# The first attention of layer 1 by sorted keys, ranks and indirect DMA in place of 512x512 numerators

## The chip, the core and the metric

The kernel runs on one core of one Trainium2 chip. The metric is the device time of one execution in microseconds, the median of the runs given; a separate, profiled execution supplies the trace. All times below are microseconds unless a row says ns.

## The reference

Input x is 32 samples of 512 nodes with 256 features; one adjacency matrix, 512x512, serves all of them. Four graph layers follow, each adding its result to x after a layer norm and a ReLU. Layer 0 is a masked attention of 4 heads, layer 2 a graph attention of 4 heads, layer 3 one of 8 heads with a prior. Layer 1, cut to what matters here:

```python
o1 = relu(h @ mlp1_w + mlp1_b)              # 512 nodes x 512 features
h1 = o1 @ W_fc
f1, f2 = h1 @ a[:512, 0], h1 @ a[512:, 0]
e = leaky_relu(f1[:, :, None] + f2[:, None, :], 0.2)   # no mask
att = softmax(e, axis=2)
out = elu(elu(att @ h1)) + o1
o3 = relu(out @ mlp2_w + mlp2_b)
# then a second graph attention of o3, masked by adj, and a residual
```

The first attention has no mask and its score depends on f1[i] + f2[j] alone. Leaky ReLU has two branches: for the nodes j with f2[j] > -f1[i] the numerator is exp(f1[i] + f2[j]), for the others exp(0.2 (f1[i] + f2[j])). Each is a product of a factor of i and a factor of j. With the nodes sorted by f2, every output row is therefore a suffix sum of one kind of weighted rows plus a prefix sum of the other, cut at the place where f2 passes -f1[i].

## The kernel before, in words

Everything is fp32; two masks are kept in bf16. A tile of 128 partitions by 512 columns is a "block" (a pool of 60), a PSUM bank holds as much (8 of them), and a sample's x is 128 x 4 x 256 (a pool of 5).

The 32 samples are not looped over on the chip. The program records the steps of all samples (class Plan, line 82 on), prices each with the function cost (line 333), and schedules them by hand: a list scheduler (order, line 169) puts every step on its engine's queue in the order of its modelled start, with due times that follow from PERIOD, the tuned numbers in URGENT, and the earliest starts in STARTS, PACE and LAYERS. At most AHEAD = 4 samples run past the oldest. What comes out is one fixed order for each of the five queues: PE (matmuls), DVE, ACT, POOL (GpSimd) and SP (which issues most DMAs). Each queue runs in order; an instruction that waits holds up all behind it. All planned instructions have line 297 in the profile, so groups are told apart by tile names.

A sample goes through these steps:

- norm_t: statistics on DVE, a power on POOL (`rs`), normalised rows `h` on ACT, eight transposes on PE, a ReLU on ACT (`hT`).
- layer 0: projections, score pairs (`sc`, two row tiles of 64 at once), Exp on ACT, mask on DVE, weighted sums in column tiles. In normalise the sums go through DRAM: `sums` to `s1` to `few`, a reciprocal, `s2`, and `rc` broadcast back.
- layer 1, first attention (first_gat). The values v = o1 W_fc are computed node by node, with f1 and f2 as two more columns (`sd`). The largest f2 is found; ew holds a factor per node for each branch; r1 spreads the i factor over all partitions. Then DVE makes the numerators p1[j, i] = max(r[i] * ew1[j], ew0[j]), four 128x512 blocks, sums them (`total`), and PE transposes the sums to get 1/sum (`rs1`, `rc`). Sixteen matmuls of 128 x 128 by 512 columns multiply v by p (`av`). elu2 applies the two ELUs with three ACT and three DVE passes over each of four blocks.
- layer 1, second attention (second_gat): masked, with numerators from ACT and DVE.
- layers 2 and 3 (separable): a row of scores per head goes to DRAM (`rd<-rT`) and comes back on all partitions (`R`, 256 KB each, 12 a sample). For each head ACT computes Exp(R + e), DVE takes a maximum and the mask (`p`), PE sums in column tiles. The sums over j are made on DVE (`total`), for one group of heads in layer 3 by POOL DMAs that add (`p<-p`).

After the last sample a few tests on the weights decide whether the result stands (`go`); otherwise a second, general program runs.

Of the kernel before, what the change touches and what calls it, by code (L numbers as in the profile page):

```python
# [14 lines left out]
I32 = mybir.dt.int32  # L15
AF = mybir.ActivationFunctionType
# [4 lines left out]
P = 128  # L21
# [20 lines left out]

PERIOD = 107.0
STARTS, PACE = (0.0, 4.0, 19.0, 123.0), 101.0
LAYERS = (0.0, 32.0, 34.0, 184.0)

URGENT = {
    "stats:0": -231, "mv:0": -37, "rs:0": -123, "ms:0": -205, "h:0": 11, "pt:0": -750, "hT:0": 14, "mm:0": -216,  # L50
    "sc:0": -122, "p0:0": -65, "total:0": -98, "av:0": 34, "sums:0": -578, "s1:0": 49, "few:0": -6, "s2:0": 16,
    "rc:0": -235, "oT:0": 85, "mv:1": -1, "rs:1": -312, "ms:1": 79, "h:1": -294, "pt:1": -8, "hT:1": 210, "o1:1": 230,
    "sd:1": -3, "v1:1": 496, "nd:1": -243, "ew:1": 150, "p1:1": 192, "total:1": -170, "sm:1": 80, "rs1:1": -271,
    "rc:1": 295, "av:1": -43, "y:1": -155, "e:1": -181, "o2:1": 223, "o3:1": 97, "v2:1": -74, "sd2:1": 230,
    "mn:1": -599, "None:1": 532, "ew2:1": 73, "p2:1": 326, "rs2:1": -12, "u:1": 67, "x:1": 261, "stats:2": 253,
    "mv:2": -2, "ve:2": -111, "rs:2": 9, "ms:2": 327, "h:2": -217, "pt:2": 246, "hT:2": -176, "mm:2": -27,
    "vs:2": -140, "es4:2": -547, "e4:2": 121, "rd:2": -46, "R:2": 10, "p3:2": -509, "av:2": -104, "total:2": -557,
    "sm:2": 273, "r4:2": -73, "ue:2": -350, "x:2": -11, "stats:3": -7, "mv:3": -124, "ve:3": 186, "rs:3": 271,
    "ms:3": -493, "pt:3": 488, "hT:3": -507, "mm:3": -191, "vs:3": -282, "es8:3": 187, "e8:3": -10, "rT:3": -676,
    "rd:3": 450, "R:3": 367, "p3:3": -733, "av:3": -428, "total:3": 545, "sm:3": -50, "sums:3": 213, "raw:3": 11,  # L60
    "s1:3": 84, "s2:3": 121, "rc:3": -208, "oT:3": 42, "None:3": 359, "af:3": 10, "top:3": 409, "ok:3": 38,
    "values:3": -217, "rows:3": 208, "gp:3": -60, "gram:3": -190, "gab:3": 123, "sq:3": -31, "tp:3": -40,
    "res:3": 224,
}
BLOCKS, KEEP = 60, 2
# [16 lines left out]
class Plan:  # L82
# [11 lines left out]
    OWN = dict(block=8, bank=2)  # L94
    SPARE = dict(block=2, bank=1)
# [28 lines left out]
    def add(self, attribute, engine, op, args, kw):  # L124
# [11 lines left out]
        reads = [v for v in list(args) + list(kw.values()) if isinstance(v, bass.AP) and not any(v is w for w in writes)]  # L136
        for ap, writing in [(v, False) for v in reads] + [(v, True) for v in writes]:
            if ap.tensor.name not in self.tile_tag:
                continue
            name, box = ap.tensor.name, extent(ap)  # L140
            if name not in step.touches:
                step.touches.append(name)
            record = self.history.setdefault(name, [])
            for other, obox, owriting in record:
                bank = writing and owriting and step.engine == other.engine == "PE"
                if (writing or owriting) and other is not step and (bank or overlap(box, obox)):
                    if other not in step.before:
                        step.before.append(other)
                        other.after.append(step)
            record.append((step, box, writing))  # L150
# [182 lines left out]
def cost(engine, op, args, kw, out):  # L333
# [22 lines left out]
    if engine == "POOL":  # L356
        if op == "dma_start":
            return 1.1, (5.2 if n == N else 8.0)
        return (1.0 if n < 16 else 0.683), 0.1
# [7 lines left out]
def gnn_stack_kernel(ctx: ExitStack, tc: tile.TileContext, a: dict, out: bass.AP):  # L367
# [47 lines left out]
    spread = const.tile([P, B], F32, name="spread")  # L415
    bq8 = const.tile([P, KD], F32, name="bq8")
# [23 lines left out]
    with prep_stack, tc.manual_schedule():  # L440
# [21 lines left out]
        nc.vector.memset(ones, 1.0)  # L462
        adjf = prep.tile([P, NT, N], F32, name="adjf", bufs=1)
# [133 lines left out]
    def pipelined(stack):  # L597
# [4 lines left out]
        q = Plan(nc, PERIOD)  # L602
        def block(name):

            return q.tile(big, [P, N], name, BLOCKS, keep=KEEP, tag="block")
# [7 lines left out]
        def small(name, *free):  # L613
            return q.tile(big, [P, *free], name, 4)

# [187 lines left out]
        def first_gat(o1):  # L803

            va, vb, sd = blocks("v1", 2), blocks("v1", 2), small("sd", NT, 2)
            for t in range(0, NT, 2):
                for i, ps in enumerate((bank("mm"), bank("mm"))):
                    for k in range(KH):
                        q.tensor.matmul(ps[:, : D + 2], o1[k][:, col(t + i)], wfc[:, k, D:], start=(k == 0), stop=(k == KH - 1))
                    q.scalar.copy(sd[:, t + i, :], ps[:, D : D + 2])  # L810
                    q.scalar.copy(half(vb, t + i), ps[:, :D])
            for t in range(0, NT, 2):
                q.scalar.copy(T(va[t // 2], "p (t d) -> p t d", d=D), node_major2(wfc[:, :, :D], t, o1))
            nd = largest(sd[:, :, 1])
            ew = small("ew", 3, NT)
            q.vector.tensor_scalar(ew[:, 2, :], sd[:, :, 0], nd[:, 0:1], 0.0, op0=ALU.add, op1=ALU.max)
            q.scalar.activation(ew[:, 2, :], ew[:, 2, :], AF.Exp, scale=ALPHA - 1.0)
            q.scalar.activation(ew[:, 0, :], sd[:, :, 1], AF.Exp, bias=nd[:, 1:2])
            q.scalar.activation(ew[:, 1, :], sd[:, :, 1], AF.Exp, bias=nd[:, 2:3], scale=ALPHA)
            r, p = on_all("r1", ew[:, 2, :]), blocks("p1", NT)  # L820
            for j in range(NT):
                q.vector.tensor_scalar(p[j], r, ew[:, 1, j : j + 1], ew[:, 0, j : j + 1], op0=ALU.mult, op1=ALU.max)
            rc = inverse_sums(p)
            o2 = blocks("o2", KH)
            for m in range(KH):
                elu2(o2[m], weighted([half(va if m < 2 else vb, j)[:, col(m % 2)] for j in range(NT)], p), rc, o1[m])
            return o2

        def second_gat(o3, xt):

            v, sd = q.tile(big, [P, NT, D + 1], "v2", 2), small("sd2", NT, 2)
            for t in range(NT):
                ps = node_major(wh, t, o3, 0, D + 2)
                q.scalar.activation(v[:, t, :D], ps[:, :D], AF.Identity, bias=ones[:, 0:1])
                q.scalar.copy(sd[:, t, :], ps[:, D : D + 2])
            q.vector.memset(v[:, :, D : D + 1], 1.0)
# [13 lines left out]
            for t in range(0, NT, 2):  # L850
                e, u, avs, rs = block("e"), block("u"), [], small("rs2", 2, 2)
                for i in range(2):
                    av = bank("av")
                    avs.append(av)
                    for j in range(NT):
                        q.tensor.matmul(
                            av[:, : D + 1], p[j][:, col(t + i)], v[:, j, :], start=(j == 0), stop=(j == NT - 1)
# [34 lines left out]
        def separable(xt, w, nh, mask, bars):  # L892
# [13 lines left out]
            rT = q.tile(big, [P, P], "rT", 4, tag="turned")  # L906
# [85 lines left out]
        def tests():  # L992
# [8 lines left out]
            for t in range(NT):  # L1001
                ai, af = q.tile(big, [P, N], "ai", BLOCKS, keep=KEEP, tag="block", dtype=I32), block("af")
# [56 lines left out]
        for i in range(B):  # L1059
# [12 lines left out]
            lambda n: big.tile([P, N], F32, tag="block", name=n, bufs=BLOCKS),  # L1072
# [3 lines left out]
        with tc.manual_schedule():  # L1076
# [6 lines left out]
            nc.vector.tensor_tensor(go1, go1, narrow[:1, :], op=ALU.mult)  # L1083
            nc.vector.tensor_copy(go, go1)

    def general(stack):
# [35 lines left out]
        small = stack.enter_context(tc.tile_pool(name="small", bufs=4))  # L1122
# [375 lines left out]
```

## Time and profile before

| | us |
|---|---|
| median of 3 runs | 3902.6 (3900.93 to 3904.77) |
| the profiled execution | 3905.73 |
| its span, first to last instruction | 3903.9 |
| PE busy | 3824.9 |
| DVE busy | 3292.2 |
| ACT busy | 2837.1 |
| POOL busy | 519.1 |
| DMA moved | 292.65 MB, mean 75 GB/s |

How to read the lines below: a group is "line engine operation out<-in, partitions x elements, xcount | busy us, mean ns of one | idle before, and what ended it". A stage row gives the stretch, its length, then busy time and count of PE, PEld (weight loads), DVE, ACT and POOL, the granted clock of PE, the share of the 16 DMA engines in use, and GB/s. A DMA queue row gives packets, MB, and the time of its packets as a share of 16 engines' span. Short instructions of PE overlap in the records, so the distance from one start to the next says more of a matmul than its mean. An fp32 matmul leaves two records.

### The profile page before, as it was taken

The numbers are of one execution on the slowest core, as the hardware profiler recorded it, in microseconds if no ns is written. First come the engines' busy times: TensorE is split into PE (matmuls) and PEld (weight loads), VectorE is DVE, ScalarE is ACT, GpSimd is POOL, SyncE is SP. The second block draws the span as 40 slices with busy tenths as digits, with TensorE's granted clock in tenths as the row PEclk, the third lists the DMA queues.
The fourth block names the chain that finished last, engine by engine and source line by source line (L and its number), as shares of the span: only waits on it lengthen the run. The fifth ranks groups of instructions, "written<-read, shape, count | busy, mean of one in ns | idle before, by whom it ended". The sixth has DMA issues, their size and how long they took to land.

```text
span 3903.9 us, 53766 instructions
## 1 busy us (share of the span) xinstructions
PE 3824.9 (98%) x17400; PEld 2230.5 (57%) x17400; DVE 3292.2 (84%) x7177; ACT 2837.1 (73%) x6128; POOL 519.1 (13%) x530
## 2 busy tenths in 40 slices
PE   8999999999999999999999999999999999999996
PEld 4555565555566555566565556565655555655643
DVE  5578988888988888988889988889888889888896
ACT  4567777777777767777677777677777777776784
POOL 0001110111110111110111111111101111101110
PEclk9999999999999999999999999999999999999998
DMA  3012331323332333332333323333323333314241
GB/s 100 19 48 61 88 93 52 92 61 82 88 84 59 93 61 82 87 76 67 82 63 89 89 66 78 81 63 88 93 58 85 70 73 88 88 55 94 46 110 48
DMA packets 217623, 292.65 MB, mean 75 GB/s; under 512 B 49915, under 2 KB 103422, under 8 KB 217334
## 3 DMA queue, kind: packets, MB, share of 16 engines
q0 software_dynamic: 68864, 111.18, 16.5%
q1 hardware_dynamic: 148196, 177.69, 14.6%
q8 instruction: 140, 2.29, 0.3%
q14 instruction: 149, 1.22, 0.1%
q10 hardware_dynamic: 274, 0.26, 0.0%
HBM read 158.79 MB, written 19.10 MB: 46 GB/s over the span
## 4 chain that ended last, share of the span: by engine, by line
PE 85%; ACT 8%; DVE 3%; issue 2%; DMA 2%; POOL 0%; SPq 0%; DVEq 0%; ACTq 0%; POOLq 0%
PE mm L297 43%; PE av L297 31%; PE pt L297 6%; ACT p L297 6%; PE sm L297 3%; DVE p L297 2%; PE sc L297 1%; DMA p<-p 1%; ACT h L297 1%; DVE total L297 1%; POOL rs L297 0%; DMA rc<-s 0%; DVE x L297 0%; DMA s<-few 0%; DVE rc L297 0%
## 5 line engine op out<-in xcount | busy, mean ns | idle before, releaser
L297 ACT ACTIVATE p<-R,e 128x512 f32<-128x512 f32 x1536 | 1001.5, 716 | 82.5 <-DVE total L297 75.6
L297 DVE SCALAR_TENSOR_TENSOR p<-p,e,mask3T 128x512 f32<-128x512 f32 x1024 | 715.0, 746 | 12.9 <-ACT p L297 12.9
L297 PE MATMUL av<-p,v 128*64 128x512 f32 (+1 forms) x2048 | 697.7, 597 | 6.6 <-ACT v L297 5.4
L297 DVE TENSOR_TENSOR total<-total,p 128x512 f32<-128x512 f32 x808 | 511.3, 686 | 0.1
L297 PE MATMUL av<-p,vs 128*32 128x512 f32 (+1 forms) x3072 | 497.9, 596 | 5.9 <-DVE p L297 5.9
L297 POOL TENSOR_TENSOR rs<-ve,mhalf 128x4 f32<-128x4 f32 x128 | 155.5, 1220 | 2367.8 <-DVE few L297 858.5
L297 POOL DMA_DIRECT2D p<-p x360 | 342.9, 1314 | 934.3 <-PE av L297 790.4
L297 PE MATMUL mm<-W_fc,o 128*128 128x256 f32 (+1 forms) x2048 | 459.5, 380 | 0.4 <-ACT o L297 0.4
L297 PEld LDWEIGHTS av<-p,v 128*64 128x64 f32 (+1 forms) x2048 | 257.6, 163 | 334.5 <-issue 278.1
L297 PEld LDWEIGHTS mm<-W_fc,o 128*128 128x128 f32 x2048 | 384.9, 190 | 83.3 <-issue 22.7
L297 DVE SCALAR_TENSOR_TENSOR p<-p,e,mask1T 128x512 f32<-128x512 f32 x512 | 352.8, 746 | 10.3 <-ACT p L297 10.1
L297 DVE TENSOR_TENSOR p<-p,mask0T 128x512 f32<-128x512 f32 x512 | 317.8, 686 | 13.9 <-ACT p L297 13.9
L297 ACT ACTIVATE h<-x,ms,rs 128x256 f32<-128x256 f32 x512 | 271.4, 593 | 69.9 <-DVE ms L297 69.8
L297 PEld LDWEIGHTS av<-p,vs 128*32 128x32 f32 (+1 forms) x3072 | 138.6, 119 | 310.0 <-issue 263.1
L297 DVE TENSOR_TENSOR total<-p,p 128x512 f32<-128x512 f32 x404 | 267.4, 690 | 39.0 <-PE av L297 22.6
L297 ACT ACTIVATE p<-sc 128x512 f32<-128x512 f32 x512 | 254.4, 673 | 3.7 <-PE sc L297 1.1
L297 PE MATMUL mm<-w,hT 128*128 128x272 f32 (+1 forms) x1024 | 253.5, 396 | 1.3 <-ACT hT L297 1.3
L297 PE MATMUL av<-v,p 128*128 128x257 f32 x1024 | 232.6, 380 | 2.7 <-ACT o L297 1.4
L297 PE MATMUL mm<-o,mlp_w 128*128 128x512 f32 x512 | 230.3, 593 | 2.1 <-DVE o L297 2.1
L297 PE MATMUL mm<-hT,mlp_w 128*128 128x512 f32 x512 | 230.9, 593 | 1.0 <-ACT hT L297 1.0
L297 PE MATMUL sc<-qT,kT 64*128 64x512 f32 x1024 | 228.9, 596 | 0.0
L297 ACT ACTIVATE e<-av,ones,rs 128x256 f32<-128x256 f32 x128 | 65.6, 562 | 220.8 <-PE av L297 108.6
(187 smaller groups left out, 5783.1 us busy)
## 6 DMA issues: line engine op xcount, KB each, us to landing
R<-rd SPq DMA_DIRECT2D x384, 256.0 KB
p<-p POOLq DMA_DIRECT2D x360, 256.0 KB, 4.9
x<-in_x_dram SPq DMA_DIRECT2D x32, 512.0 KB
x<-boa POOLq DMA_DIRECT2D x32, 512.0 KB, 6.5
rc<-s SPq DMA_DIRECT2D x128, 128.0 KB
out_dram<-x SPq DMA_DIRECT2D x32, 512.0 KB
rc<-s SPq DMA_DIRECT2D x248, 64.0 KB
s<-sums SPq DMA_DIRECT2D x94, 8.0 KB
```

Source lines behind the costliest of these rows:

```text
L297: getattr(getattr(self.nc, attribute), op)(*args, **kw)
```

## The change

The first attention no longer builds numerators. The values are written row-wise (two halves of 256 columns plus 1, then f1 and f2) into four blocks of 514 columns. The f2 of all nodes is spread over all partitions by four transposes. Eight Sign passes on ACT with summed output count, for each node, how many f2 lie below its own (its rank) and how many exceed -f1 (its cut). Four indirect DMAs on POOL scatter the rows to DRAM in rank order; SP reads them back sorted. Sums are then taken in half blocks of 64 rows: a 64x64 triangle times the weights (`w`) is multiplied with the sorted rows (`put`), in row-tiled pairs, giving within each block the suffix sums of one branch and the prefix sums of the other. ACT copies each pair's result out (`tab`) and SP writes it to a DRAM table of 513 rows, both branches side by side; the sums of the weights alone go there as single elements. The block totals are read back (`tot`), a 0/1 matrix picks the blocks before and behind the cut, and a matmul of 16 rows adds them up (`behind`). Two indirect DMAs for each of four tiles gather a table row per node by its cut; one of them adds to what is there. DVE and ACT divide and apply the ELUs row-wise, and 16 transposes bring the result back to feature-major.

A test is added that all ranks are different (`ranks`), else the general program runs. The planner prices an indirect DMA at 1.5 on POOL and 5.5 to land, and treats the two DRAM tensors as one piece each (a reader waits for all writers). The numbers of the plan are new. Blocks become 514 columns wide, and there are 62. In second_gat the values move into two such blocks.

```diff
-PERIOD = 107.0
-STARTS, PACE = (0.0, 4.0, 19.0, 123.0), 101.0
-LAYERS = (0.0, 32.0, 34.0, 184.0)
+HALF = 64
+ROW = 2 * D + 1
+PERIOD = 135.0
+STARTS, PACE = (0.0, 0.0, 7.0, 47.0), 112.0
+LAYERS = (0.0, 39.0, 87.0, 208.0)
...
-BLOCKS, KEEP = 60, 2
+BLOCKS, KEEP = 62, 2
...
+    SHARED = ("sorted", "sums_of")
...
+                if shared:
+                    clash = writing != owriting
...
+        if op == "indirect_dma_start":
+            return 1.5, 5.5
...
         def first_gat(o1):
-            va, vb, sd = blocks("v1", 2), blocks("v1", 2), small("sd", NT, 2)
...
-            r, p = on_all("r1", ew[:, 2, :]), blocks("p1", NT)
-            for j in range(NT):
-                q.vector.tensor_scalar(p[j], r, ew[:, 1, j : j + 1], ew[:, 0, j : j + 1], op0=ALU.mult, op1=ALU.max)
-            rc = inverse_sums(p)
-            o2 = blocks("o2", KH)
-            for m in range(KH):
-                elu2(o2[m], weighted([half(va if m < 2 else vb, j)[:, col(m % 2)] for j in range(NT)], p), rc, o1[m])
...
+            for t in range(NT):
+                q.tensor.transpose(pt[:, col(t)], rows[t][:, 2 * D + 1 :].to_broadcast([P, P]), ident)
+            q.vector.reduce_max(nd[:, 0:1], pt, axis=AX.X)
...
+            for i, scale in enumerate((-1.0, 1.0)):
+                for t in range(NT):
+                    q.scalar.activation(
+                        w, pt, AF.Sign, bias=rows[t][:, 2 * D + 1 - i : 2 * D + 2 - i], scale=scale,
+                        accum_out=sg[:, i, t : t + 1],
+                    )
...
+            order = q.tile(dram, [N, 2 * D + 2], "order", 6, tag="sorted")
+            for t in range(NT):
+                q.gpsimd.indirect_dma_start(
+                    out=whole(order), out_offset=bass.IndirectOffsetOnAxis(ap=at[:, 0, t : t + 1], axis=0),
+                    in_=rows[t], in_offset=None, bounds_check=N - 1, oob_is_err=False,
+                )
...
+            q.sync.dma_start(ds_, T(order[:, 2 * D + 1 :], "(t p) c -> p (t c)", p=P))
+            put = blocks("v1s", NT)
+            for t in range(NT):
+                q.sync.dma_start(put[t], order[t * P : (t + 1) * P, : 2 * D])
...
+            q.vector.tensor_tensor(
+                T(w, "p (t i c) -> p t i c", t=NT, i=2), tri[:, None, :, :].to_broadcast([P, NT, 2, HALF]),
+                T(ab, "p i t -> p t i")[:, :, :, None].to_broadcast([P, NT, 2, HALF]), op=ALU.mult,
+            )
...
+            table = q.tile(dram, [N + 1, 2 * ROW], "table", 6, tag="sums_of")
...
+            for i in range(2):
+                r = slice(i * HALF, (i + 1) * HALF)
+                q.scalar.copy(sums[r], T(sm[r, :16], "p (s i t) -> p i t s", s=2, i=2)[:, i])
+                q.sync.dma_start(
+                    of(ROW + i * (2 * ROW - 1), [2 * ROW, HALF], [HALF * 2 * ROW, 2 * NT], [1, 1]),
+                    T(sums[r], "p t s -> p (t s)")[:, :, None],
+                )
...
+            for t in range(NT):
+                tt = [bank("av"), bank("av")]
+                with q.unit("rows", 0.86):
+                    for s in range(2):
+                        r = slice(s * HALF, (s + 1) * HALF)
+                        q.tensor.matmul(tt[s], w[r, col(t)], put[t][r, :], start=True, stop=True)
+                for s in range(2):
+                    b = block("tab")
+                    q.scalar.copy(b, tt[s])
+                    q.sync.dma_start(of((2 * t + s) * HALF * 2 * ROW + ROW + 1, [2 * D, 2], [2 * ROW, HALF], [1, 2 * D]), b)
...
+            for t in range(NT):
+                q.sync.dma_start(
+                    tot[32 * t : 32 * t + 16, :],
+                    of(ROW + 1, [HALF * 2 * ROW - ROW - 1, 2], [HALF * 2 * ROW, 8], [1, 2 * D]),
+                )
+            behind = [bank("av") for _ in range(NT)]
+            with q.unit("rows", 0.86):
+                for t in range(NT):
+                    r = slice(32 * t, 32 * t + 16)
+                    q.tensor.matmul(behind[t], wt[r, :], tot[r, :], start=True, stop=True)
+            for t in range(NT):
+                g.append(wide("g1"))
+                pick = dict(
+                    out_offset=None, in_=whole(table), bounds_check=N, oob_is_err=True,
+                    in_offset=bass.IndirectOffsetOnAxis(ap=at[:, 1, t : t + 1], axis=0),
+                )
+                q.gpsimd.indirect_dma_start(out=g[t], element_offset=2 * D, **pick)
+                u.append(block("u1"))
+                q.scalar.copy(u[t], behind[t])
+                q.gpsimd.indirect_dma_start(out=u[t], compute_op=ALU.add, **pick)
...
+                q.vector.scalar_tensor_tensor(f, g[t][:, 2:], ew[:, 0, t : t + 1], f, op0=ALU.mult, op1=ALU.add)
+                q.scalar.activation(e, f, AF.Relu, bias=ones[:, 0:1], scale=rs[:, 1, t : t + 1])
+                q.scalar.activation(e, e, AF.Exp, scale=-1.0)
+                q.scalar.activation(e, e, AF.Exp, bias=mone)
+                q.vector.scalar_tensor_tensor(f, f, rs[:, 0, t : t + 1], e, op0=ALU.mult, op1=ALU.max)
+            o2 = blocks("o2", KH)
+            for m in range(KH):
+                pt = bank("pt")
+                for t in range(NT):
+                    q.tensor.transpose(pt[:, col(t)], u[t][:, col(m)], ident)
+                q.vector.tensor_tensor(o2[m], pt, o1[m], op=ALU.add)
             return o2
```

## The prediction

> **What bounds the kernel now.** I read the page's busy shares first, then the stage table, the waits, and the groups by shape inside ten periods.
>
> ```profile
> PE 3824.9 (98%) x17400; PEld 2230.5 (57%) x17400; DVE 3292.2 (84%) x7177; ACT 2837.1 (73%) x6128; POOL 519.1 (13%) x530
> ...
> q0 software_dynamic: 68864, 111.18, 16.5%
> q1 hardware_dynamic: 148196, 177.69, 14.6%
> ```
>
> TensorE is busy almost throughout; the 16 DMA engines have about 31% of work. In the chain of work the same PE piece (mm, 16 records, 6.87 us) starts at 1509.27 and again at 1626.87, so I cut ten periods of 117.6 us out of the steady part:
>
> ```profile
> 1509.27:2685.27 1176.00, 1168.69 (x5328) 685.67 (x5331) 1020.08 (x2216) 878.43 (x1905) 163.82 (x167) 1.00 0.33 77
> ```
>
> Columns: length, then PE, PEld, DVE, ACT, POOL busy. Per sample: PE 116.9 of 117.6, DVE 102.0, ACT 87.8, POOL 16.4. The clock is 1.00. So one sample costs what its matmuls cost; 32 x 117.6 = 3763, and the other 141 us of the 3903.9 span are the pipeline's head and tail (PE's largest single wait, 25.5 us in all, is for ACT h). The profiled execution took 3905.7, 1.8 more than its span and 3.1 more than the median.
>
> **What the change takes from PE.** Ten periods hold:
>
> ```profile
> L297 PE MATMUL av<-p,v 128*128 128x512 f32 x320 | 142.7, 593 | 1.0 <-ACT v L297 1.0
> ...
> L297 PE MATMUL sm<-ident,total 128*128 128x128 f32 x40 | 6.0, 273 | 0.0
> L297 PE MATMUL pt<-ident,rs 128*128 128x128 f32 x40 | 6.0, 273 | 0.0
> ```
>
> An fp32 matmul leaves two records, so 320 are 16 matmuls a sample. In the order of time 24 of them take 10.30 us to the next instruction, 0.86 a matmul: 13.7 us a sample. Thirteen transposes also go (sums, their spread, r1, the maximum), 0.11 apart in a run: 1.4. Removed: 15.1.
>
> Added, per sample: four row-tiled pairs, 64 rows each, at the 0.88 of the score pairs, which have that shape (32 records in 7.07 us): 3.6. Four 16-row matmuls on four row groups: 0.9 if they run together as the four 32-column `sm` matmuls do (8 records in 0.9), 3.4 if one by one; I take 0.9, since the layout is the same turned round. Four matmuls of 8 columns at 0.22 (the eight one-column matmuls of L540 leave 16 records in 1.8 us): 0.9. Twenty-one transposes at 0.11: 2.3. Changes of array mode: 0.5, an estimate (four at the 0.13 that lies free ahead of the first score pair at 1573.86). Sum 8.2. Net: 7 us a sample off PE, 224 in all.
>
> **What it adds to DVE and ACT.** DVE loses 14.0 (four p at 0.55, three totals and a reduction at 0.69, twelve y/o passes at 0.69, small ones) and gains 15.6 (eight scalar_tensor_tensor at 0.75, four PSUM adds, w and the maximum at 0.69, some 35 small ones at 0.15 to 0.23): about 103.5. ACT loses 13 and gains 28: eight Sign passes at 0.7 to 0.8 (row `p<-R,e` 716 ns, plus the sum written out), twelve copies at 0.58, eight biased 256-column copies at 0.49, the exponentials as before: about 102. In a period of 110.6 both would be at 92 to 94%. Nothing before shows three engines so full; between 0 and 6 us a sample lost to their in-order queues I take 2, because DVE at 87% cost PE only 0.7 us. Without other losses: 3903.9 - 224 + 64 + some 15 for a longer tail = 3759 of span.
>
> Bounding the unseen: Sign could need another table than Exp (each load 1283 ns in the page's ACT rows, two or more a sample), but Relu, Identity, Copy and Exp alternate here with no load between; I take 0.
>
> **POOL.** Twelve indirect DMAs a sample are new. Nearest rows: an ordinary 128-row DMA there.
>
> ```profile
> 1506.39 3.57 POOL L297 DMA_DIRECT2D p<-p  x4 [23.99 <-PE av L297]
> 1510.22 0.89 POOL L297 DMA_DIRECT2D p<-p  x1 [0.25 <-DVE total L297]
> ```
>
> By these 0.9 to 1.3 each, 11 to 16 us a sample on an engine with 16.4 of 117.6 used. [...] I take 1.5, by the row.
>
> **DMA: where I expect the loss.** Bytes are no problem: about 17 us a sample of work on each of the 16 engines (160 rows of 2 KB for scatter, reads and gathers at 0.1, half that again for the adding ones at 0.18, 1536 four-byte pieces). The eight `tab` writes are different. Each stores 128 rows of 2 KB, and its DRAM side is [2, 64, 512], outermost count 2. Two candidates for their price. By size the row is `R<-rd`: 256 KB, 128 packets of 2 KB at 84 (median) to 101 ns (mean) over 16 engines, under 1 us. By shape it is this one:
>
> ```profile
> rd<-rT SPq DMA_DIRECT2D x32, 8.0 KB
> rd<-rT SPq DMA_DIRECT2D x32, 16.0 KB
> ```
>
> Its DRAM side has 4 token blocks outermost. In the trace's packet records every DMA ends with one four-byte packet per engine it used: a load of x leaves 16, the 16 KB `rd<-rT` at 1583.0 leaves 4, and its 32 packets of 25 to 42 ns take 0.30 us, some 3.2 at a time. [...] So I take the row by shape: 64 rows x 84 to 101 ns = 5.4 to 6.5 us a DMA, and since all eight share two engines, 43 to 52 us a sample one after the other. With the 36.6 those engines have now (31.1% of 117.6), the 17, and the reads of `tot` (also 2 engines, 3), they would be busy 100 to 109 us of a period: not above it, but a queue.
>
> What waits: the reads of `tot` (SP), the gathers (POOL), by whole tensor, so for the last `tab`. Behind the wait on SP's in-order queue stand R, s, few and rc of the other samples; on POOL the `rs` power of every norm and the `p<-p` sums; on PE the `behind` matmuls and all after them. The plan prices each `tab` at 0.4 + 3.4 + 1.4 us side by side; with eight copies at 0.58 before them it expects the table about 10 us after the first copy. With 43 to 52 of own work, stretched by other traffic on those engines, I put the real end at 55: 45 late. How much the static order absorbs is read from a chain of before: the exponentials of ew end at 1617.7, PE turns them at 1626.2, 9 us; R that landed at 1586 to 1595 is first used at 1592.3, later heads wait up to 20. So 5 to 20 at a hop; over the two or three hops here 10 to 30; I take 17. Left: 28 us a sample that PE stands still (10 to 40). It comes back every period, since nothing lets PE pass a waiting instruction.
>
> Removed waits go nowhere useful: the old chain (r1, totals, sums, rc) cost PE almost nothing.
>
> **Sum.** Period 117.6 - 7 + 2 + 28 = 140.6; x 32 = 4499; head and tail 141 + 15: 4655 of span. Outside it 1.8, against the median -3.1: about 4650.
>
> **Rivals.**
> 1. *The table writes stall everything* (forecast, 55%): 4650; with 15 to 42 us left, 4240 to 5100.
> 2. *PE gets its 7 us* (29%): 3757. The writes spread over more engines than the row by shape says, or the order leaves some 40 us between table and use. For it: PE is the bound today, and each sample lives some 585 us between load of x and store (load at 1576.8 follows the store of five samples before at 1573.9), so there is queueing to be eaten. It decides when less than 5 us of lateness is left over. Against it: the four packets of `rd<-rT`. Range 3650 to 3880.
> [...]
> 4. *The chain's other hops or full ACT and DVE eat the gain* (8%): 7 to 15 us a sample lost, 3900 to 4100.
>
> **Numbers.** This kernel's measurement tells about 0.2% from no change. Slower: 55 + 8 + 6 (of case 4) = 69%; same 3% (2 of case 4, 1 of case 2); faster 28%. Likeliest case alone: 4240 to 5100. The range 3700 to 5000 leaves out some 5% of case 2 below, and about 10% of cases 1 and 3 above.
>
> **What would show it.** `tab` writes taking 5 us each and landing one after the other, two completion packets each; PE waits in `av<-wt,tot` or in what follows it, 10 to 40 us each period, charged to a DMA; SP and POOL waiting for table<-tab; PE busy near 80%. PE busy time down by about 220 us shows the first sum right either way. [...] Wrong in another way: two equal keys would send the program into its slower general path behind this one, above my range.

## The result, and the profile after

The changed kernel takes 5530.7 (median of 4 runs, 5525.6 to 5537.7): 1.417 times the time before (95% interval 1.4148 to 1.4197), 1628 more. The forecast was 4650 with a range to 5000: the sign and the place were right, the loss was 2.2 times what its own sum had (747).

The page after, the lines that answer to those of before, and the row of granted clock:

```profile
PE 4002.1 (72%) x17659; PEld 2274.8 (41%) x17659; DVE 3271.1 (59%) x7905; ACT 3235.7 (59%) x7120; POOL 1033.3 (19%) x922
...
PEclk9787889798878978897989789888979897888878
...
q0 software_dynamic: 107776, 212.13, 19.9%
q1 hardware_dynamic: 253540, 282.89, 16.7%
```

PE's share falls from 98% to 72% although no other engine is above 59%: nothing is full, so something is waited for. The clock of PE, 1.00 in the steady part before, is now 0.7 to 0.9 in every slice. A stretch of 2000 us out of the middle (length, then PE, PEld, DVE, ACT, POOL busy with their counts, clock, DMA share, GB/s):

```profile
1000.00:3000.00 2000.00, 1470.75 (x6477) 839.42 (x6477) 1215.16 (x2912) 1198.49 (x2645) 396.42 (x347) 0.85 0.38 92
```

The same stretch of the kernel before:

```profile
1000.00:3000.00 2000.00, 1987.48 (x9082) 1163.67 (x9082) 1734.88 (x3765) 1494.24 (x3234) 283.84 (x289) 1.00 0.33 77
```

The DMA engines as a whole are at 0.38, before at 0.33: bytes are not the limit. The waits of the kernel after (who waited, for whom: us in all, times, the longest):

```profile
...
POOL g L309 <- DMA table<-tab: 611.1, 12, 53.9
...
PE pt L309 <- ACT h L309: 463.0, 60, 28.5
PE av L309 <- DMA tot<-table: 451.2, 17, 43.5
...
ACT p L309 <- DMA table<-tab: 384.9, 35, 30.4
DVE ms L309 <- POOL rs L309: 288.5, 76, 20.2
PE mm L309 <- DVE oT L309: 188.8, 13, 21.0
```

The forecast's wait is there: PE stands at `av<-wt,tot` 17 times, 26.5 on average and up to 43.5. But it is less than a third of the idle time.

PE waits as long for `h`, the head of other layers of other samples. Followed back in the trace, these 60 waits have two main sources. In 23 of them, 191 us, ACT waited for DVE's `ms`, which waits for POOL's `rs`, and POOL stands before a gather. In 9 others, 256 us, ACT stood ahead of `h` before an Exp that makes `p`, until a `tab` had landed. That Exp does not read the table. But `p` and `tab` are blocks of the same pool, and the Exp starts within 0.1 us of the landing: the block it needs is held by the write. Its row on the page:

```profile
L309 ACT ACTIVATE p<-R,e 128x512 f32<-128x512 f32 x1536 | 1021.4, 728 | 400.6 <-DMA table<-tab 329.1
```

In the kernel before the same row has 82.5 us of idle time, none of it for a write to DRAM. Last, PE waits for `oT`, a product that comes back through DRAM on SP's queue. SP's queue in one such stretch (start, length, what it issues):

```profile
2017.87 10.15 SPq L309 DMA_DIRECT2D table<-tab  x4
2042.84 2.55 SPq L309 DMA_DIRECT2D tot<-table  x4
...
2061.96 39.44 SPq L309 DMA_DIRECT2D table<-tab  x8
2116.53 2.50 SPq L309 DMA_DIRECT2D tot<-table  x4
```

and PE in the same stretch, its three long waits (in brackets the idle time ahead of the row and what ended it):

```profile
2018.78 2.04 PE L309 MATMUL mm<-L_WoT,oT 128*128 128x256 f32 x4 [21.02 <-DVE oT L309]
2046.81 0.69 PE L309 MATMUL pt<-ident,h 128*128 128x128 f32 x2 [17.98 <-ACT h L309]
...
2119.56 2.74 PE L309 MATMUL av<-tot,wt 16*128 16x512 f32 x4 [39.65 <-DMA tot<-table]
```

The eight writes of one sample hold SP for 39.44, 4.9 each. That is near the length of the transfer itself (the completion packets of these eight come in pairs, one pair every 5.56 us), and not what an issue needs: the fastest of this row takes 482 ns, the median 4970 (shortest, median and longest in the line below). All 256 issues together take 951 us, 30 a sample.

```profile
L309 SPq DMA_DIRECT2D table<-tab x256: 482/4970/10885, 168.3 to 5319.3; - x128
```

In the trace's packet records 2.1 packets are under way at a time during such a burst, 57 or 58 packets of 2 KB in 2.5 us, and each write leaves two completion packets. That is two engines: the row by shape was the right one. Only when the last write lands, at 2116, can SP issue the read of `tot` and whatever stands behind it.

The loss can be divided without any experiment. The span of PE is its idle time, plus its work at full clock, plus what the half clock costs (half of the busy time spent at half clock, from the trace's clock records, which know only 0.5 and 1; in the kernel after the records of `mm<-wvT,hT`, 256 columns, start 427 ns apart at 0.5 and 216 at 1, medians):

| us | before | forecast | after |
|---|---|---|---|
| PE idle | 79.0 | 1054 | 1528.7 |
| PE's work at full clock | 3811.3 | 3587 | 3707.0 |
| cost of the half clock | 13.7 | 14 | 295.0 |
| span | 3903.9 | 4655 | 5530.7 |

The forecast column is the prediction's own sum in these terms (idle 79 + 32 x 30 + 15; work 3811 - 224). Of the 876 that it lacks, 475 are idle time, 281 the clock, and 120 PE's work. The row of work is the least firm: runs below with the same matmuls in another order come out between 3695 (scatters_apart) and 3903 (no_urgencies).

### The profile page after: what moved, and what is told of

It reads as the page before. It is cut to its first block, busy times and chain, and to the rows that moved or that the text cites. A ratio compares the mean times of both kernels' runs of the same rounds, so it can differ in the third digit from the quotient of the medians.

```text
span 5530.7 us, 58740 instructions
## 1 busy us (share of the span) xinstructions
PE 4002.1 (72%) x17659; PEld 2274.8 (41%) x17659; DVE 3271.1 (59%) x7905; ACT 3235.7 (59%) x7120; POOL 1033.3 (19%) x922
## 2 busy tenths in 40 slices
DMA packets 361915, 499.12 MB, mean 90 GB/s; under 512 B 110203, under 2 KB 163710, under 8 KB 361590
## 5 line engine op out<-in xcount | busy, mean ns | idle before, releaser
L309 PE MATMUL av<-p,vs 128*32 128x512 f32 (+1 forms) x3072 | 570.5, 633 | 89.7 <-DVE p L309 86.3
L309 PE MATMUL pt<-ident,h 128*128 128x128 f32 x1024 | 196.3, 308 | 464.3 <-ACT h L309 463.0
L309 PE MATMUL mm<-W_fc,o 128*128 128x256 f32 (+1 forms) x2048 | 489.2, 389 | 0.0
L309 POOL DMA_INDIRECT g<-table,at x128 | 154.2, 1204 | 1761.4 <-DMA table<-tab 611.1
L309 DVE TENSOR_TENSOR total<-total,p 128x512 f32<-128x512 f32 x744 | 479.0, 682 | 0.1
L309 PE MATMUL av<-tot,wt 16*128 16x512 f32 x256 | 96.7, 869 | 477.2 <-DMA tot<-table 451.2
L309 PEld LDWEIGHTS mm<-W_fc,o 128*128 128x128 f32 x2048 | 387.3, 195 | 71.2 <-issue 14.8
L309 PEld LDWEIGHTS pt<-ident,h 128*128 128x128 f32 x1024 | 132.6, 155 | 581.2 <-ACT h L309 512.2
L309 DVE SCALAR_TENSOR_TENSOR rs<-g,ew 128x1 f32<-128x1 f32 x128 | 27.4, 215 | 540.5 <-DMA g<-table,at 494.2
L309 POOL DMA_INDIRECT order<-v,at x128 | 149.8, 1170 | 806.5 <-DVE ew L309 226.2
L309 PE MATMUL sc<-qT,kT 64*128 64x512 f32 x1024 | 266.6, 645 | 16.9 <-ACT vs L309 12.9
```

Source lines behind the costliest of these rows:

```text
L309: getattr(getattr(self.nc, attribute), op)(*args, **kw)
```

## The experiments

Theory A: the table writes, on two engines, hold SP's queue, and all that stands behind them waits, whether it reads the table or not. Rival B: the longer chain of hops through DRAM and POOL, with a fuller ACT and DVE, would have cost the same with any writes. Rival C: the planner does not know these prices, and an order that knew them would absorb the writes.

All runs, beside the kernel before on the same chip (3900.5 to 3905.4 in the different groups). table_not_awaited, order_not_awaited, scatters_apart, apart_narrow and the two runs named norms_off_pool leave out part of the work or of its data, as is said with each.

| run | us | ratio to before |
|---|---|---|
| tab_on_16 | 4473.1 | 1.146 (1.1441 to 1.1479) |
| half_on_16 | 4934.6 | one run |
| before_two_engines | 5097.0 | one run |
| before_16_engines | 3906.0 | one run |
| table_not_awaited | 4427.3 | one run |
| order_not_awaited | 4329.9 | one run |
| scatters_apart | 4264.0 | one run |
| plan_knows_price | 5288.6 | one run |
| plan_knows_scatters | 4614.2 | 1.182 (1.1776 to 1.1871) |
| slower_starts | 4603.2 | 1.181 (1.1786 to 1.1831) |
| no_urgencies | 4845.2 | 1.243 (1.2409 to 1.2460) |
| before_no_urgencies | 4246.5 | 1.089 (1.0868 to 1.0905) |
| norms_off_pool | 4557.3 | 1.167 (1.1647 to 1.1686) |
| before_norms_off_pool | 3899.1 | 0.999 (0.9985 to 0.9999) |
| apart_narrow | 4237.1 | 1.086 (1.0840 to 1.0876) |
| before_h_twice | 4183.8 | 1.072 (1.0700 to 1.0736) |
| plan_knows_sign | 4739.8 | 1.215 (1.2133 to 1.2174) |

### The writes, cut in two

tab_on_16 writes the same bytes to the same places in the same order, each block as two transfers of 64 partitions; half_on_16 does so for every second block.

```diff
-q.sync.dma_start(of(..., [2 * D, 2], [2 * ROW, HALF], [1, 2 * D]), b)
+for i in range(2):
+    q.sync.dma_start(of(... + i * 2 * D, [2 * ROW, HALF], [1, 2 * D]), b[i * HALF : (i + 1) * HALF, :])
```

> The changed kernel with each of the eight table writes cut into two DMAs of 64 partitions (outermost count 64 on both sides), in the same place of the same order; nothing else. Theory A (the writes with outermost count 2 run on two DMA engines, and their queue of 43 us a sample holds up SP, the table's readers and through them all else): most of the loss goes, 3700 to 4000 us, granted clock back above 0.97, two tab packets streams replaced by 16. Rival B (the loss lies in the chain's other hops and in the new order: scatter, sorted read, gathers, POOL's waits): the time stays above 4700.

> The changed kernel with four of the eight table writes cut as in the run before, the other four as they were. Theory A, with some lateness absorbed by the order: clearly nearer to the cut version than half way, 4100 to 4600. If the loss is proportional to the time that two engines are busy: about half way between the cut version and 5531, near 4650. Rival B: above 5100.

Measured 4473.1: the cut gives back 1058 of the 1628. Half of the writes cut (4934.6) gives 596, about in proportion. Both missed the ranges of either theory, and the clock came back to 0.93 only, not over 0.97. A half block leaves 16 completion packets (the page counts 117884 packets under 512 B, against 110203: 7681 more, where 512 x 16 - 256 x 2 makes 7680), SP's issue of it has a median of 552 ns, and the long waits of PE shown above shrink to these:

```profile
PE av L309 <- DMA tot<-table: 72.1, 19, 10.0
...
PE pt L309 <- ACT h L309: 66.6, 49, 8.6
...
PE mm L309 <- DVE oT L309: 53.1, 13, 9.8
```

All three fell together, the two that do not read the table too: 451 to 72, 463 to 67, 189 to 53; ACT's wait for a `tab` before `p` went from 385 to 17. So the shape of the writes is the cause of this part. How it divides over SP's queue, the two engines and the held blocks the run does not tell. It leaves 571 unexplained. In the account by PE (a profiled span of 4485) they are 433 more idle time and 241 more half clock than before, less 93 of work.

### The same writes in the kernel before

before_two_engines adds eight such writes a sample to the old first attention; nobody reads them. before_16_engines moves the same bytes in sixteen transfers of 64 partitions.

```diff
+spare = q.tile(dram, [N + 1, 4 * D + 2], "spare", 6)
+for n in range(8):
+    ...
+    q.sync.dma_start(bass.AP(..., ap=[[2 * D, 2], [4 * D + 2, 64], [1, 2 * D]]), b)
```

> The kernel before with eight more writes of 256 KB a sample from its value blocks into a DRAM tensor that nobody reads, each with outermost count 2 on the DRAM side. Theory A in full (the queue of the two engines holds SP and all transfers behind it, even with no reader): 4050 to 4800. Only the readers of the table lose: under 3960.

> The same bytes from the same blocks to the same places, as 16 DMAs of 64 partitions a sample. Theory A: 3890 to 3960 (some 7 us of SP issue and 2 MB a sample on 16 engines, both hidden). If bytes and not the engine count make the loss: as slow as the run with outermost count 2.

Measured 5097.0 and 3906.0: 1195 us more for writes without a reader, and no more than a few us when the same bytes go in transfers of 64 partitions. SP with the one and the other, in the same part of the program:

```profile
2074.95 42.84 SPq L297 DMA_DIRECT2D spare<-v  x8
2117.88 5.39 SPq L297 DMA_DIRECT2D s<-sums  x1
```

```profile
2079.91 12.54 SPq L297 DMA_DIRECT2D spare<-v  x16
2095.25 0.52 SPq L297 DMA_DIRECT2D s<-sums  x1
```

`s<-sums` is a step of another sample's softmax, a transfer of 8 KB; its issue alone takes 5.39 behind the writes, 0.52 without them. In the first kernel ACT has made `sums` at 2090.3: the transfer stands 27.6 on SP's queue, and the issue that waits for its landing (`few<-s`) follows 14.8 after its start, 1.7 in the second. The waits of before_two_engines show how it reaches PE:

```profile
PE sm L297 <- DVE total L297: 1046.2, 29, 38.0
DVE p L297 <- DMA s<-sums: 1041.7, 28, 39.0
```

All 28 of these waits of DVE stand before `p<-r,ew`, a numerator of the first attention, 37.0 each in the most. It does not read `s`; it needs a block, and in the kernel's text `sums` lies in a block of the same pool, which is free when `s<-sums` has read it. PE then waits for the `total` behind it on DVE's queue. No reader of the written data is needed: SP's queue and a block that comes free late are enough. Rival B can't explain this, since nothing of the sorting is in this kernel. In the account by PE 1109 us are more idle time and 81 more half clock. The size was missed (at most 4800 was expected). The same writes on another engine's queue, which would part the hold of SP from the two engines, were not tried.

### The hops, no longer awaited

Three kernels on top of tab_on_16, each with the previous one's edit too; they no longer compute the attention. `tot` and the gathers read a table filled once before the loop; then `put` and `ds` read rows filled once; then each of the four scatters writes a tensor of its own.

```diff
-in_=whole(table)
+in_=whole(fixed["table"])
...
-q.sync.dma_start(put[t], order[t * P : (t + 1) * P, : 2 * D])
+q.sync.dma_start(put[t], fixed["order"][t * P : (t + 1) * P, : 2 * D])
...
-out=whole(order)
+out=whole(apart[t])
```

> The version with cut table writes (4473 us), its order unchanged, but tot and both gathers read a DRAM tensor of ones filled at the start instead of the table; the table is still written in full. It leaves out that the prefix sums reach the output. If what is left of the loss (571 us against before) is the wait from the table writes to their readers: 3950 to 4150. If it lies in the scatter and the sorted read, or in POOL: above 4300.

> As the run before, and the sorted rows too are read from a tensor of ones (the scatters are still issued). It leaves out both round trips through DRAM as waits. If the second half of the remaining loss is the wait from scatter to sorted read: 200 to 350 us less than the run before it. If little: within 60 us of it.

> As the run before, and each of the four scatters writes a DRAM tensor of its own, so none waits for the one ahead of it on POOL (2.5 us each in the trace). Leaves out both round trips and joins no sorted rows. Theory: with all DRAM waits gone only the fixed order and the fuller engines are left: 3850 to 4000, PE clock above 0.98. If above 4150, the order itself (or ACT and DVE) is at fault, not the round trips.

Measured 4427.3, 4329.9 and 4264.0: 46, 97 and 66, one run each. The three waits of a reader for a writer that the new attention is built on cost 209 together, less than any of the expectations that put the loss there, and 361 are left. Only the writers are no longer awaited: the reads themselves are still made on SP's and POOL's queues, and PE waits for `tot` about as long as in tab_on_16 (72.1):

```profile
PE av L314 <- DMA tot<-fixed_table: 70.2, 18, 9.4
```

In the account by PE, scatters_apart has 391.6 idle, 3694.6 of work and 176.0 of half clock. Its page:

```profile
PE 3870.6 (91%) x17659; PEld 2226.1 (52%) x17659; DVE 3260.7 (77%) x7905; ACT 3222.7 (76%) x7120; POOL 1109.5 (26%) x922
```

### A planner that knows

plan_knows_price tells the planner that the changed kernel's write holds SP for 5.0, as the trace shows, and lands 3.4 later, and lays the order anew. (The 3.4 is short for eight in a row: in the kernel after, `tot` is issued 15.0 us, in the median, after the last write's issue ended.)

```diff
+    if out.tensor.name.startswith("table") and len(out.ap) == 3 and out.ap[0][1] == 2 and out.ap[1][1] == HALF:
+        return 5.0, 3.4
```

> The changed kernel with its two-engine table writes as they are; only the planner's price of such a write is changed, from 0.4 us of SP and 4.8 to land to 5.0 of SP and 3.4 more, so that the order is made for what the chip does. Prediction's view (lateness that the order doesn't know): 4100 to 4700, much of the loss returned, since two engines with 100 to 109 us of work a sample are not yet the bound. If the queue itself is the loss: within 5% of 5531.

Measured 5288.6, within the 5% that were expected if the queue itself is the loss: 242 of 1628 come back. But the trace does not bear this reading out. In the new order the writes seldom stand in a row (their issues take 0.54 in the median), and PE's wait for `tot` is down from 451 to 48. In its place PE waits for `p` 282 us, before 103, and for `u` 111, before 60. So an order can take the writes out of each other's way, and this one loses elsewhere most of what it wins. Rival C is not settled by it: the planner's table of urgencies stayed as it was, and one fitted to the new prices was not tried.

The last 361 were then looked for in the order of tab_on_16. plan_knows_scatters prices a scatter at 3.6 + 2.2 in place of 1.5 + 5.5 and the pair of table writes at 1.1 of SP in place of 0.4, slower_starts also lets a sample start every 124 us, plan_knows_sign (alone, on tab_on_16) prices the Sign pass at 0.95 in place of 0.66.

```diff
-            return 1.5, 5.5
+            return (3.6, 2.2) if out.tensor.name.startswith("order") else (1.5, 5.5)
...
-STARTS, PACE = (0.0, 0.0, 7.0, 47.0), 112.0
+STARTS, PACE = (0.0, 0.0, 7.0, 47.0), 124.0
...
-        return busy + (0.093 if "accum_out" in kw else 0.0), 0.12
+        return busy + (0.38 if "accum_out" in kw else 0.0), 0.12
```

> The kernel with its table rows written by 64-partition transfers (the earlier run tab_on_16: 4473.1 us), with two of the planner's prices set to what the trace of that run shows: a scatter of a block's rows 3.6 us of POOL and 2.2 us to landing (each waits for the one before it to land), where the plan had 1.5 and 5.5; and the pair of table writes 1.1 us of SP, where it had 0.4. The whole list of work is then laid anew; the work itself is untouched. Theory A (about 210 of the 571 us that tab_on_16 still loses to the kernel before are waits for transfers that the order allows too little time, and the other 360 are an order that pays for it in PE gaps and in the half clock after them): an order that knows the prices wins back a part, 50 to 200 us: 4270 to 4420. Rival (the loss is ACT and DVE, too full to feed PE in any order): within 30 us of 4473.

> The same kernel as plan_knows_scatters, with one number more changed: the plan lets a sample start every 124 us instead of every 112. PE's own work is some 116 us a sample at full clock, so a pace of 112 starts samples ahead of what PE can finish, and a pace of 124 leaves each sample's chain some time over. If the order is what costs (theory A), a looser pace gives back part of the gaps: below plan_knows_scatters by 30 to 150 us. If samples in flight are what hides the hops through DRAM, a looser pace takes cover away and the time rises. The floor by the pace itself is about 31 x 124 + 250 = 4090, if the plan's clock held.

> tab_on_16 (4473.1 us) with one price of the planner corrected: a Sign pass with its sum written out takes 707 + 224 ns in the trace, 0.93 us, where the plan had 0.66; it gets 0.95 now. The work is the same, the list is laid anew. before_h_twice showed that 9.4 us of ACT work a sample that the order doesn't know of cost 8.8 us a sample. If these 8 x 0.28 = 2.2 us a sample are paid in the same way, an order that knows them wins 70 us: 4380 to 4440. Rival (an order laid for prices near these carries a fitted table of urgencies, and any new price loses more of its fit than it wins, as plan_knows_scatters did by 141 us): 4473 to 4700.

All three are slower than the 4473.1 that they started from: 4614.2, 4603.2, 4739.8; the slower starts moved the time by 11, no more than these runs scatter. Better prices beside an unchanged table of urgencies made worse orders, so in this form the theory fell. What an order is worth is told by two more, with the table of urgencies emptied:

```diff
-URGENT = {
-...
-}
+URGENT = {}
```

> The same kernel as plan_knows_scatters, with the table of urgencies by kind and layer emptied (all zero), so that the planner orders the steps by its own chains of prices alone. Beside it runs the kernel before with its own table emptied. If the change's table of urgencies does for it what the other table does for the kernel before, both lose alike without it. Theory A: the kernel before loses more (100 us and over) than this one (under 100 us, or even a gain), since this table was laid for prices that the chip doesn't keep.

> The kernel before with its table of urgencies by kind and layer emptied, nothing else. It tells how much of the time before rests on this table: theory A says 100 to 500 us (so that an order alone can be worth what tab_on_16 still loses), the rival (order is worth little here, ACT and DVE set the rest) says under 50 us: 3900 to 3950.

The kernel before loses 346 without its table, plan_knows_scatters loses 231. The table laid for a kernel is worth hundreds of us to it (under 100 was expected for the sorted version), and a price changed beside it may lose some of that. The distance between the two kernels without tables is 4845.2 - 4246.5 = 599; with them it is 571 (tab_on_16) or 714 (plan_knows_scatters, which has the same prices as no_urgencies). So the fit of this table alone does not make the distance. The other numbers tuned for each plan (PERIOD, STARTS, LAYERS) stayed, and what a full fit would give is open.

### POOL, ACT and DVE

norms_off_pool is tab_on_16 with a constant written by DVE where POOL computed the power of each norm (the division by the standard deviation is left out), the rest of the work and the order as they were; before_norms_off_pool is its control.

```diff
-q.gpsimd.tensor_tensor(rs, ve, mhalf, op=ALU.pow)
+nc.vector.tensor_scalar(rs, ve, 0.0, 0.25, op0=ALU.mult, op1=ALU.add)
```

> [...] Theory C (POOL's in-order queue, now with scatters and gathers that wait for DRAM, holds the norms of the other samples: DVE's ms waits 145.9 us for POOL's rs in tab_on_16, 55.1 in the kernel before): the time falls by the difference and what follows from it in the half clock, 90 to 200 us: 4270 to 4380. Rival (POOL's waits are cover time and PE waits elsewhere): within 40 us, 4430 to 4500.

> The control for norms_off_pool: the kernel before with the same edit (rs a constant written by DVE, the division by the standard deviation left out). Both theories: POOL has 13% of work there and DVE's ms waits 1.2 us at a time for it, so 3880 to 3910.

Measured 4557.3, 84 slower and outside both ranges, with the control unmoved at 3899.1. Taking the norms off POOL's queue gives nothing back as this order stands. Why it got slower was not settled; `ACT ab <- DMA ds<-order` went from 103.6 to 202.8 in it, so one wait may hide behind another.

apart_narrow is scatters_apart with 16 columns in place of 512 in eight ACT copies and eight DVE passes a sample (the other columns are left out); before_h_twice is the kernel before with each ACT pass that makes `h` done twice.

```diff
-q.scalar.copy(b, tt[s])
+nc.scalar.copy(b[:, :16], tt[s][:, :16])
```

```diff
-nc.scalar.activation(half(h, t), xt[:, t, :], AF.Identity, ...)
+for _ in range(2):
+    nc.scalar.activation(half(h, t), xt[:, t, :], AF.Identity, ...)
```

> scatters_apart (4263.96 us: no table, no order and no landing of the scatter before is awaited) with part of the new attention's ACT and DVE work made 16 columns wide instead of 512: the eight copies of tab on ACT (some 0.45 us less each, 3.6 a sample; the table gets rows of a mask instead) and eight passes over u on DVE (some 0.6 less each, 4.8 a sample), so most columns of these steps are left out. Order and everything else are the same. Theory B (ACT and DVE are too full, what is left is their work): 3.6 to 8.4 us a sample come back, 115 to 270: 3995 to 4150. Rival (latency and order, not the amount of work): the chain of a sample grows shorter by these 8 us too, but its cover was enough or lies elsewhere: 4220 to 4264.

> The kernel before with each of the sixteen 256-column passes a sample that make h on ACT done twice into the same place, the order as it is: ACT 87.8 + 16 x 0.55 = 96.6 us of a period of 117.6, near the 102 that the change gives it. Theory B (an ACT at over 80% starves PE): each head gets 2.2 us longer and ACT's queue fuller, 100 to 300 us more: 4005 to 4200. Rival (ACT's load costs nothing by itself while the order leaves room): below 3950.

apart_narrow took 98.7 us of work off ACT and 125.8 off DVE and gave back 27, against a single run. before_h_twice put 299.8 us on ACT, which had 73% of work, and the time rose by 281; in the account by PE 160 of it is idle time, 62 the half clock and 56 work. Its page and the wait that grew, 25.5 in the kernel before:

```profile
PE 3942.6 (94%) x17400; PEld 2255.9 (54%) x17400; DVE 3292.4 (79%) x7177; ACT 3136.9 (75%) x6640; POOL 521.3 (12%) x530
```

```profile
PE pt L301 <- ACT h L644: 176.9, 283, 7.1
```

The two answer each other: in a fixed order, work that was added ahead of PE's largest wait was paid almost in full on an engine a quarter idle, and work taken away from other steps gave back little. How much of the last 361 is such lengthened steps, how much the reads through DRAM and how much the order stays open; the runs say that eight copies and passes are some 27 of it.

## Why the prediction was wrong, by its own steps

**DMA: where I expect the loss.** The choice of the row by shape was right: two engines, a write every 5.56 us, one after the other (5.4 to 6.5 said), two completion packets each. That such a write gets two engines, and all eight of a sample the same two, which the 43 to 52 us of the sum rest on, no run of the kernel before shows: it was the author's estimate. In the kernel after eight such writes in a row took 8 x 5.56 = 44.5. **The term that failed is "Left: 28 us a sample that PE stands still".** PE's idle time grew by 1450 / 32 = 45.3 a sample, against 30 in the sum. It took 45 us of lateness at the readers of the table and subtracted 17 of slack at this one place. But the lateness reaches PE by more ways than these readers. The issues themselves hold SP for 30 us a sample that the plan priced at 8 x 0.4 = 3.2, so everything behind them is late before anybody has waited for the table; and a block that a `tab` gives back late keeps ACT before an Exp of another sample. The stretch above has three waits of PE, 21, 18 and 40, where the forecast had one. Over the run 451 us of its idle time are at `tot`, 256 behind that Exp, 191 behind POOL's gathers and 189 at `oT`; slack at one of these places does not help the others. before_two_engines shows the ways without a reader by themselves: 1195. The list of what stands behind SP's wait (R, s, few, rc) was in the prediction; it was named and not priced, and the blocks were not named.

**The clock.** The second step that failed: the sum has no term for it, so it stood at nothing, without a reason. The half clock costs 295, 281 more than before. The steps from a long wait, out of the windows of the kernel after (columns as in the stretch above):

```profile
2100.00:2104.00 4.00, 0.00 (x0) 0.00 (x0) 0.00 (x0) 0.00 (x0) 0.00 (x0) 0.50 0.13 47
2119.60:2122.60 3.00, 2.70 (x4) 0.92 (x4) 0.22 (x1) 0.85 (x2) 2.39 (x3) 0.50 0.73 194
...
2125.60:2128.60 3.00, 3.00 (x8) 0.52 (x6) 1.90 (x3) 2.20 (x4) 2.42 (x2) 0.50 0.69 135
2128.60:2131.60 3.00, 2.78 (x14) 1.99 (x12) 1.42 (x3) 2.49 (x5) 1.57 (x1) 0.57 1.09 268
```

PE works again from 2119.6, at half clock until 2131. The kernel before has 7 stretches at half clock, at its head and its tail, which cost 13.7, some 2 each. One such stretch a sample would have cost 32 x 2 = 64 (an estimate from these), so a forecast of 28 us of standing a sample had a number to add. The trace after has 91 gaps of PE over 3.4 us (3.41 is the step in which its clock records change) and 107 stretches at half clock, together 1741 us, 590 of them with PE busy.

**What the change takes from PE.** Nearly right. Counted in both traces at full clock (each record up to the start of the next, time at half clock by half), the rows that go take 490 us and the rows that come 283: 207 less, where the sum had 224. The sign that was named for it, PE busy down by about 220, could not show: PE's busy time rose by 177, with 295 of half clock in it. Rows of the kernel after:

```profile
L309 PE MATMUL av<-v1s,w 64*128 64x512 f32 x512 | 120.3, 610 | 0.0
L309 PE MATMUL pt<-ident,u 128*128 128x128 f32 x512 | 97.0, 342 | 60.8 <-DVE u L309 60.0 <-DVE o L309 0.6
L309 PE MATMUL av<-tot,wt 16*128 16x512 f32 x256 | 96.7, 869 | 477.2 <-DMA tot<-table 451.2 <-ACT p L309 22.7 <-ACT u L309 2.0
```

The four 16-row matmuls (the last row) take 96.7 / 32 = 3.0 a sample, which looks like the upper bound of 3.4. But 74 of the 96.7 are at half clock. Where their data is there in time, at 1323.9, the eight records start in two groups of four, each group within 0.02 us, and are done in 1.14: they do run together, near the 0.9 that was taken. The rest of the 120 that the sum was short of, 103, is on matmuls that both kernels have, most of it on tiled ones (19 on `av<-p,vs` with 32 columns, 14 on the score pairs).

**POOL.** Right: 1170, 1204 and 1652 ns for scatter, gather and adding gather, near the 1.5 taken by the row. With POOL busy 19% of the span, the case that it becomes the bound (8%) fell. On POOL's queue what costs is the wait: a scatter waits for the one before it to land (`POOL order <- DMA order<-v,at`: 118.0, 40 times), and with that wait gone scatters_apart gained 66.

**What it adds to DVE and ACT.** The sizes held: DVE 3271 / 32 = 102.2 against 103.5, ACT 101.1 against 102; no table load for Sign shows (5 table loads in ACT's rows, as in the kernel before). The loss of 2 us a sample that was put on them can't be told apart from the 361 that stay open.

**Rival 4** (hops and full engines) had 8% and 7 to 15 us a sample. With the writes repaired it comes out as 571 / 32 = 17.8, what the matmuls give back already taken off; 6.5 of it are the awaited hops. That is over its range, and it was a rival to be added to case 1, not one in its place.

## What to carry to other kernels

A write whose DRAM side had outermost count 2 cost three times here: its own time on two engines (5.56 us), the queue that issues it (4.9) with everything behind it, and the block that it held until it landed. Ask of each transfer how many engines it gets, of each queue how long an issue holds it, and of each buffer who wants it next, before asking who reads the data. Cutting each write in two gave back 1058 of 1628 us with the order unchanged. When PE will stand still, add the half clock to the sum (295 us here). And in an order laid by hand take idle share for no slack: 300 us of work added ahead of PE's largest wait cost 281, on an engine at 73%.

## What the runs showed of the hardware beyond that

- An issue on SP's queue takes 0.6 us for a transfer of 64 partitions (552 and 595 ns median, tab_on_16 and before_16_engines) and about 5 when eight in a row go to the same two engines (4970 and 5240 ns median, kernel after and before_two_engines, up to 18.1 us). That the issuer is held because those engines' queue is full is a reading of these numbers, not something a record shows.
- PE's clock falls 3.2 us (median of 69 in the kernel after) after a gap of over 3.4 us begins and is full again 4.9 us (median of 70, 2.6 to 11.7) after PE resumes; 31 of its 107 stretches at half clock have no gap over 3.4 us in them or in the 4 us before, only shorter ones. Of the 14 longest returns (8.5 us and more) 13 have the 16-row matmuls among their first work, as in the rows above; two that were transposes alone took 3.2 and 3.5. Whether it is the 16 rows was not tried.
- No order of the sorted version that was run beat the kernel before. The rows that it changes on PE are worth 207 us, 5.3% of the time, and every version lost more to waits and the half clock.
